# Layer 0 of a graph network: eight blocks per node tile divided anew between ScalarE and VectorE

## The chip, the cores and the metric

The kernel runs on one core of one Trainium2 chip. The metric is the device time of one execution in microseconds (us), as a median of three runs. Engine names follow the profile: PE is TensorE's matrix multiply and PEld its weight load, DVE is VectorE, ACT is ScalarE, POOL is GpSimd, SP is the queue of SyncE, which here only issues transfers. Unless a unit stands beside it, a time is in us.

## The reference, cut to what matters

Two layers of a graph network run over 8 batches, 2048 nodes and 64 features, all in float32. Layer 0 gives every node weights of its own, mixed from 16 matrices by the node's embedding.

```python
# layer 0: x (8, 2048, 64), A (2048, 2048), embedding (2048, 16), weight (16, 3, 64, 64)
w = einsum('nd,dkio->nkio', embedding, weight)
b = einsum('nd,do->no', embedding, bias)
As = [I, A, 2.0 * (A @ A) - I]
x_g = einsum('knm,bmc->bnkc', stack(As), x)
x = layernorm(x + einsum('bnki,nkio->bno', x_g, w) + b)
# layer 1: both supports are A
x1 = A @ x;  x2 = 2.0 * (A @ x1) - x
x = layernorm(x + concat([x, x1, x2, x1, x2]) @ weight1 + bias1)
```

The kernel takes x, A·x and A·(A·x) as its three operands of layer 0 and folds the 2 and the minus sign into the weights. It relies on the pattern of the matrix (every nonzero of a row has one value) and has a general path beside it for other matrices, which does not run on these inputs.

## The kernel before, in words

**Stages.** Four multiplications with the matrix ("hops") surround layer 0. The first hop (L254) takes the matrix in quarters and keeps sums of them. The second hop and the third are done by `seven_products` (L586), seven products of quarter size with eight steps each (L664). Between them stands layer 0, one tile of 128 nodes after the other, 16 tiles. The fourth hop (`hop_g`, `hop_tile`) and the last layer norm end the kernel.

**Operands of layer 0.** [...] every operand is divided into three parts: a high part, a low part and a mixed part. `parts` (L309) does that: ACT casts the high part (L312), DVE subtracts for the low part (L314), and the mixed part is made in one of two ways. With `quick` DVE does it in one instruction (L317); without, ACT scales the high part (L319) and POOL adds the low one (L320). `operands` (L725) prepares a tile's three operands: x (`of_x`, loaded as `xt`), the first hop (`of_hop`, after TensorE has transposed it, L300), and the second hop (`of_second`). Each is a generator that issues one step whenever it is called, and the tile before calls them.

**Blocks.** `mix0` (L402) runs eight blocks a tile. A block fills two banks of PSUM: `bank` (L84) takes one of four such pairs in turn, as they come free. There are two kinds of block.
- `by_batch` (L417), called for `(g, 0)` and `(g, 1)`: one pair of batches, eight of the 16 embedding entries, 18 matmuls of 512 columns. ACT evicts it in eight instructions of 128 elements, each scaled by the node's embedding entry, into tiles called `aside` (L423). When both blocks of `g` are there, POOL sums the aside tiles in three halvings (`sum_aside`, L440) and adds them to the sum `acc` (`add_aside`, L445).
- `by_four` (L425), called for `(g, 2)` to `(g, 5)`: two pairs of batches, four embedding entries, 36 matmuls of 256 columns. DVE evicts it in four instructions of 256 elements, each of which multiplies by the embedding entry and adds into `acc` (L433).

The loop over tiles gives the order of blocks in `pieces`, and in `at` the other work that is recorded ahead of each block. Tiles 0 to 14 have two blocks by batch and six by four, the last tile four and four:

```python
pieces = [(0, 0), (0, 4), (0, 5), (1, 2), (0, 1), (1, 3), (1, 4), (1, 5)]
```

**Order.** While layer 0 is recorded, the list `in_order` is set, and each engine keeps its instructions in the order in which they are recorded. `n1`, `n2`, `n3` are the steps of the previous tile's layer norm (L359: DVE sums and scales, POOL centres, ACT squares, DVE sums, ACT takes the root, DVE inverts, POOL normalises). `times_r` (L712) and `begin_sum` (L389) are POOL work for later tiles. `transpose` (L303) turns the previous tile's normalised values over for `project` (L458), which runs at a tile's end with two pairs of banks, and ACT copies its results out (L475).

**Third hop.** In `seven_products` the first step takes four pairs of banks, two for even products and two for odd ones:

```python
sums.extend([bank("accT") for _ in range(2)] for _ in range(2))
```

**Pools.** `RAW` buffers (5) hold raw matrix slabs, aside tiles and one pair of low and mixed parts a tile. `HL` buffers (8) hold high and low parts. `load_weights` puts layer 0's weights into raw buffers too.

Of the kernel before, what the change touches and what calls it, by code (L numbers as in the profile page):

```python
# [18 lines left out]
P = 128  # L19
B, N, C = 8, 2048, 64  # L20
NT = N // P
D = 16
DG = 4
EPS = 1e-5
FIRST = 8
HL = 8
RAW = 5
WARM = 12
SLOTS = 3
SPLIT = 4096.0  # L30
# [9 lines left out]
def pattern(  # L40
# [43 lines left out]
    def bank(name):  # L84

        return psum.tile([P, 2, 512], F32, tag="ps", name=name)
# [40 lines left out]
    def ordered(ins):  # L127
        if in_order:
            tc.keep_in_program_order(ins)
# [16 lines left out]

    def node_bias(pb):

        eT, b0_sb = bias_sb[:, : N // 4], bias_sb[:, N // 4 :]
        for j in range(4):  # L150
            for g in range(4):
                q = slice(32 * g, 32 * g + D)
                nc.tensor.matmul(  # L153
                    pb[g // 2][:, g % 2, j * C : (j + 1) * C], lhsT=eT[q, j * P : (j + 1) * P], rhs=b0_sb[q],
                    start=True, stop=True, tile_position=(32 * g, 0),
                )
# [2 lines left out]
        to = ebias[:, 8 * h : 8 * h + 8, :].rearrange("p (g t) c -> p g (t c)", g=2)  # L159
        ordered(nc.vector.tensor_copy(to, pb[h][:, :, : 4 * C]))  # L160

    wl = work2.tile([P, 5, C], F32, tag="t0", name="wl")
    bias_sb = work2.tile([P, N // 4 + C], F32, tag="t0", name="bias_sb")

    loads = [(bias_sb, bias), (pack_sb, pack[:, : NT * D]), (wl.rearrange("p k o -> p (k o)"), pack[:, NT * D + C :])]
    loads += [(bias1, pack[:, NT * D : NT * D + C]), (rrow, diag.to_broadcast([P, N]))]

    def weights():
# [230 lines left out]

    def mix0(t, tt, acc, at, pieces):  # L402

        def block(pm, lhsT, ds):
            for k in range(3):
                for n in range(3):
                    for j in range(2):
                        q = slice(j * C, (j + 1) * C)
                        nc.tensor.matmul(  # L409
                            pm[:, j], lhsT=tt[k][n][q, lhsT, :], rhs=w_parts[n][k][q, ds, :],  # L410
                            start=(k == 0 and n == 0), stop=(k == 2 and n == 2),
                        )

        def e(d):
            return emb_sb[:, t, d : d + 1]

        def by_batch(g, i):  # L417
            pm = bank("pm").rearrange("p j (d c) -> p j d c", c=C)
            block(pm, 2 * g + i, slice(0, 2 * DG))
            if i == 0:  # L420
                aside[g] = [rawp.tile([P, DG, 2, 2, C], F32, tag="raw", name="aside") for _ in range(2)]
            for d in range(2 * DG):
                ordered(nc.scalar.activation(aside[g][d // DG][:, d % DG, :, i, :], pm[:, :, d, :], AF.Copy, scale=e(d)))  # L423

        def by_four(g, dg):  # L425
            dg -= 2
            pm = bank("pm").rearrange("p j (i d c) -> p j i d c", i=2, d=DG)
            for i in range(2):
                block(pm[:, :, i], 2 * g + i, slice(dg * DG, (dg + 1) * DG))
            for d in range(DG):  # L430
                part = acc[:, 4 * g : 4 * g + 4, :]
                got = pm[:, :, :, d, :].rearrange("p j i c -> p (j i) c")
                ordered(nc.vector.scalar_tensor_tensor(part, got, e(dg * DG + d), part, ALU.mult, ALU.add))  # L433

        aside = {}

        def sum_aside(g):
            one, other = [a.rearrange("p d j i c -> p d (j i) c") for a in aside[g]]
            for to, more in ((one, other), (one[:, :2], one[:, 2:]), (one[:, 0], one[:, 1])):
                ordered(nc.gpsimd.tensor_tensor(to, to, more, ALU.add))  # L440

        def add_aside(g):
            part = acc[:, 4 * g : 4 * g + 4, :]
            one = aside[g][0][:, 0].rearrange("p j i c -> p (j i) c")
            ordered(nc.gpsimd.tensor_tensor(part, part, one, ALU.add))  # L445

        for n, (g, i) in enumerate([*pieces, (None, None)]):
            for work_here in at[n]:
                if isinstance(work_here, tuple):
                    for part in work_here[0]:  # L450
                        {"sum": sum_aside, "add": add_aside}[part](work_here[1])
                else:
                    work_here()
            if n < len(pieces):
                (by_batch if i < 2 else by_four)(g, i)
        return layernorm(acc)
# [126 lines left out]
        (S4, "B22", (0, 1)), ((0, 1), "B21", (0, 0)), ((1, 1), "T4", (1, 0)),  # L583
    )

    def seven_products(s, to, sums, more, wait=4, raw=()):  # L586

# [28 lines left out]
        def step(p, kk):  # L618
# [37 lines left out]

            def use(got):
                if p == 0 and kk == 0:
                    sums.extend([bank("accT") for _ in range(2)] for _ in range(2))
                acc, hl, S = sums[p % 2], got["hl"], got["s"]  # L660
                for i in range(2):
                    for h in range(2):
                        for c in range(2):
                            nc.tensor.matmul(  # L664
                                acc[i][:, c], lhsT=hl[h][:, i * P : (i + 1) * P], rhs=S[:, c * 512 : (c + 1) * 512],
                                start=(kk == 0 and h == 0), stop=(kk == KK - 1 and h == 1),
                            )
                if p == 3:
                    sum_of_y(kk, "T4")
                for f in more.get((p, kk), ()):  # L670
                    f()
                if kk < KK - 1:
                    return
                if p < 6:
                    todo.extend([nothing] * wait)
                for i in range(2):
                    for c in range(2):
                        todo.append(lambda i=i, c=c: put(acc[i][:, c], i, c))
                while p == 6 and todo:
                    todo.pop(0)()  # L680
                todo.extend(more.get(p, ()))
# [40 lines left out]
    def by_pair(a):  # L722
        return a.rearrange("p (j n) -> p j n", n=P)

    def operands(t, quick=False):  # L725

        xt = work2.tile([P, B // 2, P], F32, tag="t0", name="xt")
        load(nc.sync, xt, xT[t])
        tt = [None] * 3

        def begin(k, src):
            where, tag = ((rawp, "raw"), (spool, "s"))[k != 2]
            high = hpool.tile([P, B // 2, P], F32R, tag="hl", name="hl")
            pair = where.tile([P, 2, B // 2, P], F32R, tag=tag, name="parts")
            tt[k] = [high, pair[:, 0], pair[:, 1]]
            return parts(src, tt[k], by_half if k == 1 else lambda to: to, quick)

        def of_x():
            yield from begin(0, xt)

        def of_hop(pt=None):
            yield from begin(1, transposed(z[1][t], pt))

        def of_second():
            yield from begin(2, by_pair(z[2][t]))

        return tt, of_x(), of_hop, of_second()

# [74 lines left out]
    def quarter_back(a, b, which):  # L823
# [11 lines left out]
        (0, 6): [last_projected],  # L835
        **{(2 + t // KK, t % KK): [lambda t=t: add_bias(t)] for t in range(NT)},
        3: quarter_back(1, 1, 1), 4: quarter_back(0, 1, 0), 5: quarter_back(0, 0, 1),
    }, wait=2)

    third_got = {}  # L840

# [15 lines left out]
    for t in range(NT):  # L857
# [4 lines left out]
        if not last:  # L862
            following, of_x, of_hop, of_second = coming
            of_hop = of_hop()
            at[1] += [go(of_x)] * (1 if t else 3)
            at[2] += [go(of_hop), n1, go(of_hop), go(of_hop), n2]
            if t + 2 < NT:
                at[2] += [lambda: times_r(t + 2)]
                at[4] += [lambda: got.update(coming=operands(t + 2))]
            at[3] += [n3, go(of_second), lambda: got.update(acc=begin_sum(t + 1))]  # L870
            at[4] += [go(of_second), go(of_second)]
            at[6] += [(("sum", "add"), 0)]
            at[7] += [lambda: got.update(hT=transpose(h, "hT"))] if t else []
            pieces = [(0, 0), (0, 4), (0, 5), (1, 2), (0, 1), (1, 3), (1, 4), (1, 5)]
        else:
            at[1] += [n1, n2]
            at[2] += [n3, lambda: early(0, "y_high", *s)]
            at[3] += [(("sum",), 0), lambda: early(0, "y_low")]
            at[4] += [lambda: early(1, "y_high", *s)]
            at[5] += [lambda: early(1, "y_low")]  # L880
            at[6] += [(("add",), 0), lambda: got.update(hT=transpose(h, "hT")), lambda: early(2, "y_high")]
            at[7] += [(("sum",), 1), lambda: early(2, "y_low"), lambda: early(3, "y_high")]
            at[8] += [(("add",), 1), lambda: early(3, "y_low")]
            pieces = [(0, 0), (0, 1), (0, 4), (1, 0), (0, 5), (1, 1), (1, 4), (1, 5)]
        norm_now = mix0(t, tt, acc, at, pieces)
        if t:
            project(t - 1, got["hT"])
        if "coming" in got:
# [487 lines left out]
```

## Time and profile before

| What | Value |
|---|---|
| Three runs | 763.59, 763.61, 765.11; median 763.61 |
| Profiled execution, its own time | 764.04 |
| Its span, first to last instruction | 762.3 |
| Granted TensorE clock | 0.999 |
| Busy over the span | PE 753.6, PEld 660.6, DVE 560.2, ACT 406.7, POOL 269.7 |
| Busy in one steady tile of layer 0, 395.20 to 414.16 | PE 18.96, DVE 15.26, ACT 10.68, POOL 15.12 |
| DVE evictions in layer 0 (L433) | 376 of 482 ns, busy 181.0 |
| ACT evictions in layer 0 (L423) | 272, busy 74.0 |
| Start of the third hop on PE | 527.69 |

The span is what the trace covers; about 1.7 lie around it. Busy time is the union of an engine's instructions. The mean of one instruction can be longer than its share of busy time, because neighbours overlap: 272 evictions on ACT have a mean of 383 ns but are busy 74.0, so 272 ns each. Lines of the profile are those of the kernel before; the change adds lines, so L409 becomes L410 and L433 becomes L439 later on.

### The profile page before, as it was taken

To read this page: it belongs to the slowest core of one execution; us is meant where nothing else is said; L and a number is where in the kernel's file an instruction comes from. 1 tells how busy PE (TensorE), PEld (TensorE's weight loads), DVE (VectorE), ACT (ScalarE), POOL (GpSimd) and SP (SyncE) were. 2 spreads that over 40 slices of the span, in tenths; PEclk is the share of its full clock that TensorE was granted. 3 is DMA by queue.
4 is the path that set the end of the run, shared out by engine and by line. 5 is a ranking of instruction groups with operands and counts; after the bars stand their busy time and mean duration, and the time that the engine had idled before them with its cause. 6 is when DMAs were issued, how large, how long until landed. Compare 5 with 4: busy or idle time off the path is not lost.

```text
span 762.3 us, 16926 instructions
## 1 busy us (share of the span) xinstructions
PE 753.6 (99%) x6634; PEld 660.6 (87%) x6634; DVE 560.2 (73%) x1159; ACT 406.7 (53%) x896; POOL 269.7 (35%) x297
## 2 busy tenths in 40 slices
PE   9999999999999999999999999999999999999996
PEld 6888888888889999999999999998888888888885
DVE  6768867678757888888888888877688648668663
ACT  5456533877745555555555555558887663112111
POOL 0000000000026877777777777777100000011441
PEclk9999999999999999999999999999999999999999
DMA  8998996555520000000000000003454444565631
GB/s 325 346 393 282 350 312 233 154 177 162 171 69 17 20 20 15 20 18 16 16 16 17 15 16 3 2 16 87 135 167 151 130 154 142 175 177 175 208 127 46
DMA packets 73558, 96.69 MB, mean 127 GB/s; under 512 B 4864, under 2 KB 48384, under 8 KB 73344
## 3 DMA queue, kind: packets, MB, share of 16 engines
q1 hardware_dynamic: 62064, 76.66, 31.8%
q10 hardware_dynamic: 11408, 18.89, 6.6%
q8 instruction: 54, 0.88, 0.5%
q14 instruction: 32, 0.26, 0.1%
HBM read 76.65 MB, written 18.87 MB: 125 GB/s over the span
## 4 chain that ended last, share of the span: by engine, by line
PE 98%; DVE 1%; issue 0%; ACT 0%; DVEq 0%
PE pm L409 36%; PE accT L664 27%; PE acc L254 15%; PE a L254 10%; PE accT L254 6%; PE pu L466 2%; PE pt L300 1%; PE first L143 1%; PE accT L814 1%; DVE acc L433 1%; PE accT L466 0%; PE accT L153 0%; PE accT L300 0%; ACT sq L994 0%; DVE z L289 0%
## 5 line engine op out<-in xcount | busy, mean ns | idle before, releaser
L433 DVE SCALAR_TENSOR_TENSOR acc<-pm,pack_sb,acc 128x256 f32<-128x256 f32 x376 | 181.0, 482 | 44.0 <-PE pm L409 32.0
L409 PE MATMUL pm<-wh,hl 64*128 64x512 f32 (+1 forms) x1332 | 208.0, 303 | 0.0
L664 PE MATMUL accT<-s,hl 128*128 128x512 f32 x896 | 205.9, 390 | 0.8 <-DVE acc L433 0.8
L409 PE MATMUL pm<-wm,parts 64*128 64x512 f32 (+1 forms) x1332 | 203.5, 296 | 0.0
L409 PE MATMUL pm<-wl,parts 64*128 64x512 f32 (+1 forms) x1332 | 203.4, 296 | 0.0
L664 PEld LDWEIGHTS accT<-s,hl 128*128 128x128 f32 x896 | 167.5, 188 | 36.5 <-issue 1.6
L409 PEld LDWEIGHTS pm<-wh,hl 64*128 64x128 f32 x1332 | 130.9, 187 | 4.0 <-issue 0.4
L409 PEld LDWEIGHTS pm<-wl,parts 64*128 64x128 f32 x1332 | 130.8, 187 | 3.7
L409 PEld LDWEIGHTS pm<-wm,parts 64*128 64x128 f32 x1332 | 130.5, 187 | 3.8
L652 ACT CAST s<-raw 128x1024 fp32r<-128x1024 bf16 x104 | 109.9, 1057 | 37.9 <-ACT hl L234 23.4
L254 PE MATMUL acc<-hl,s 128*128 128x512 f32 x512 | 116.8, 390 | 0.0
L254 PEld LDWEIGHTS acc<-hl,s 128*128 128x128 f32 x512 | 96.2, 188 | 20.5 <-issue 0.3
L423 ACT ACTIVATE aside<-pm,pack_sb 128x128 f32<-128x128 f32 x272 | 74.0, 383 | 48.9 <-PE pm L409 48.1
L715 POOL TENSOR_TENSOR z<-z,rrow 128x512 f32<-128x512 f32 x16 | 21.1, 1320 | 212.4 <-DVE z L688 212.4
L234 ACT CAST hl<-z 128x256 fp32r<-128x256 f32 (+1 forms) x96 | 47.7, 515 | 60.1 <-PE acc L254 24.1
L440 POOL TENSOR_TENSOR aside<-aside 128x1024 f32<-128x1024 f32 (+2 forms) x51 | 75.3, 1476 | 4.2 <-ACT aside L423 1.6
L254 PE MATMUL a<-hl,s 128*128 128x512 f32 (+1 forms) x352 | 73.4, 370 | 0.0
L254 PEld LDWEIGHTS a<-hl,s 128*128 128x128 f32 x352 | 61.9, 188 | 11.3
L320 POOL TENSOR_TENSOR parts<-parts 128x512 fp32r<-128x512 f32 x45 | 58.2, 1294 | 35.1 <-DVE parts L314 27.5
L238 DVE TENSOR_TENSOR hl<-z,hl 128x512 fp32r<-128x512 f32 (+1 forms) x96 | 54.7, 577 | 12.9 <-ACT hl L234 10.1
L287 POOL TENSOR_TENSOR z<-z,got 128x512 f32<-128x512 f32 x3 | 4.8, 1631 | 144.4 <-ACT got L286 144.4
L254 PE MATMUL accT<-hl,s 128*128 128x512 f32 x192 | 44.3, 390 | 0.0
(136 smaller groups left out, 814.4 us busy)
## 6 DMA issues: line engine op xcount, KB each, us to landing
raw<-in_adj SPq DMA_DIRECT2D x58, 512.0 KB, 6.1
raw<-sums_of SPq DMA_DIRECT2D x64, 256.0 KB, 2.9
sums_of<-z ACTq DMA_DIRECT2D x16, 512.0 KB, 6.6
raw<-quarters SPq DMA_DIRECT2D x32, 256.0 KB, 2.7
raw<-in_adj SPq DMA_DIRECT2D x16, 384.0 KB, 3.5
quarters<-seen ACTq DMA_DIRECT2D x16, 256.0 KB, 5.8
xt<-in_xT SPq DMA_DIRECT2D x16, 256.0 KB, 2.7
z<-in_x SPq DMA_DIRECT2D x15, 256.0 KB, 6.8
```

The lines of the kernel that those rows point to most:

```text
L234: ordered(nc.scalar.copy(to[0], src))
L238: ordered(nc.vector.tensor_tensor(to[1], src, to[0], ALU.subtract))
L254: nc.tensor.matmul(accs[i], lhsT=s[:, i * P : (i + 1) * P], rhs=hl[h], start=(first and h == 0), stop=(last and h == 1),)
L320: ordered(nc.gpsimd.tensor_tensor(mixed, mixed, low, ALU.add))
L409: nc.tensor.matmul(pm[:, j], lhsT=tt[k][n][q, lhsT, :], rhs=w_parts[n][k][q, ds, :], start=(k == 0 and n == 0), stop=(k == 2 and n == 2),)
L423: ordered(nc.scalar.activation(aside[g][d // DG][:, d % DG, :, i, :], pm[:, :, d, :], AF.Copy, scale=e(d)))
L433: ordered(nc.vector.scalar_tensor_tensor(part, got, e(dg * DG + d), part, ALU.mult, ALU.add))
L440: ordered(nc.gpsimd.tensor_tensor(to, to, more, ALU.add))
L466: nc.tensor.matmul(pm[:, j, i * 3 * C : (i + 1) * 3 * C], lhsT=hT[q, 2 * g + i, :], rhs=v[q], start=True, stop=True,)
L652: ordered(nc.scalar.copy(s, got["raw"]))
L664: nc.tensor.matmul(acc[i][:, c], lhsT=hl[h][:, i * P : (i + 1) * P], rhs=S[:, c * 512 : (c + 1) * 512], start=(kk == 0 and h == 0), stop=( ...
L715: ordered(nc.gpsimd.tensor_tensor(to, to, r, ALU.mult))
```

## The change

Tiles 0 to 14 now have four blocks by batch and four by four. The blocks by batch of the second quarter of the batches and embedding entries (`g` = 1) go the new way: `mix0` gets `on_vector`, and for a `g` in it each block has one aside tile of its own, from which a single DVE reduce sums the eight entries over the outer axis, read with a step of 128 elements (`reduce_aside`). A DVE addition then adds the sums of both blocks to `acc` (`add_reduced`). The blocks by batch of `g` = 0 are summed on POOL as before. The last tile is as it was.

The mixed parts of x and of the second hop are always made by DVE (`quick`). The order of blocks and of the other work changes in tiles 0 to 14. In the third hop, the even products get the first and third pair of banks, the odd ones the second and fourth. `HL` is 7 and `RAW` is 6. The node bias is loaded in two transfers, the small one into a sixth slice of `wl`.

```diff
-HL = 8
-RAW = 5
+HL = 7
+RAW = 6
...
-    loads = [(bias_sb, bias), (pack_sb, pack[:, : NT * D]), (wl.rearrange("p k o -> p (k o)"), pack[:, NT * D + C :])]
+    loads = [(bias_sb, bias[:, : N // 4]), (wl[:, 5], bias[:, N // 4 :]), (pack_sb, pack[:, : NT * D])]
+    loads += [(wl[:, :5].rearrange("p k o -> p (k o)"), pack[:, NT * D + C :])]
...
-            if i == 0:
-                aside[g] = [rawp.tile([P, DG, 2, 2, C], F32, tag="raw", name="aside") for _ in range(2)]
+            if g in on_vector:
+                aside[g, i] = rawp.tile([P, 2 * DG, 2, C], F32, tag="raw", name="aside")
+                to = [aside[g, i][:, d] for d in range(2 * DG)]
+            else:
+                if i == 0:
+                    aside[g] = [rawp.tile([P, DG, 2, 2, C], F32, tag="raw", name="aside") for _ in range(2)]
+                to = [aside[g][d // DG][:, d % DG, :, i, :] for d in range(2 * DG)]
...
+        def reduce_aside(i):
+            if i == 0:
+                aside["sum"] = xcpool.tile([P, 2, 2, C], F32, tag="ln_xc", name="both")
+            src = aside[1, i].rearrange("p d j c -> p (j c) d")
+            to = aside["sum"][:, i].rearrange("p j c -> p (j c)")
+            ordered(nc.vector.tensor_reduce(to, src, AX.X, ALU.add))
+
+        def add_reduced(_):
+            part = acc[:, 4:8, :].rearrange("p (j i) c -> p i j c", j=2)
+            ordered(nc.vector.tensor_tensor(part, part, aside["sum"], ALU.add))
...
-                    sums.extend([bank("accT") for _ in range(2)] for _ in range(2))
+                    four = [bank("accT") for _ in range(4)]
+                    sums.extend([four[a], four[b]] for a, b in pairs)
...
-            yield from begin(0, xt)
+            yield from begin(0, xt, True)
...
-            yield from begin(2, by_pair(z[2][t]))
+            yield from begin(2, by_pair(z[2][t]), True)
...
-    }, wait=2)
+    }, wait=2, pairs=((0, 2), (1, 3)))
...
-            at[2] += [go(of_hop), n1, go(of_hop), go(of_hop), n2]
+            at[1] += [n1, lambda: got.update(acc=begin_sum(t + 1))]
             if t + 2 < NT:
-                at[2] += [lambda: times_r(t + 2)]
+                at[1] += [lambda: times_r(t + 2)]
+            at[1] += [n2, go(of_hop)]
+            at[2] += [n3, (("reduce",), 0), go(of_hop)]
+            at[4] += [go(of_hop), go(of_second)]
+            if t + 2 < NT:
                 at[4] += [lambda: got.update(coming=operands(t + 2))]
-            at[3] += [n3, go(of_second), lambda: got.update(acc=begin_sum(t + 1))]
-            at[4] += [go(of_second), go(of_second)]
-            at[6] += [(("sum", "add"), 0)]
+            at[5] += [(("reduce",), 1), (("add_reduced",), 1), go(of_second)]
+            at[6] += [(("sum",), 0)]
             at[7] += [lambda: got.update(hT=transpose(h, "hT"))] if t else []
-            pieces = [(0, 0), (0, 4), (0, 5), (1, 2), (0, 1), (1, 3), (1, 4), (1, 5)]
+            at[7] += [go(of_second)]
+            at[8] += [(("add",), 0)]
+            pieces, on_vector = [(1, 0), (0, 4), (1, 1), (0, 0), (0, 5), (0, 1), (1, 4), (1, 5)], (1,)
```

More of the change, by code (lines that the diff above doesn't have):

```diff
@@ L147, in node_bias @@
     def node_bias(pb):
-        eT, b0_sb = bias_sb[:, : N // 4], bias_sb[:, N // 4 :]
+        eT, b0_sb = bias_sb, wl[:, 5]
         for j in range(4):
@@ L160, in keep_node_bias @@
         ordered(nc.vector.tensor_copy(to, pb[h][:, :, : 4 * C]))
-    wl = work2.tile([P, 5, C], F32, tag="t0", name="wl")
-    bias_sb = work2.tile([P, N // 4 + C], F32, tag="t0", name="bias_sb")
-    loads = [(bias_sb, bias), (pack_sb, pack[:, : NT * D]), (wl.rearrange("p k o -> p (k o)"), pack[:, NT * D + C :])]
+    wl = work2.tile([P, 6, C], F32, tag="t0", name="wl")
+    bias_sb = work2.tile([P, N // 4], F32, tag="t0", name="bias_sb")
+    loads = [(bias_sb, bias[:, : N // 4]), (wl[:, 5], bias[:, N // 4 :]), (pack_sb, pack[:, : NT * D])]
+    loads += [(wl[:, :5].rearrange("p k o -> p (k o)"), pack[:, NT * D + C :])]
     loads += [(bias1, pack[:, NT * D : NT * D + C]), (rrow, diag.to_broadcast([P, N]))]
@@ L398, in begin_sum, with mix0 @@
         return acc
-    def mix0(t, tt, acc, at, pieces):
+    def mix0(t, tt, acc, at, pieces, on_vector=()):
         def block(pm, lhsT, ds):
@@ L419, in by_batch @@
             block(pm, 2 * g + i, slice(0, 2 * DG))
-            if i == 0:
-                aside[g] = [rawp.tile([P, DG, 2, 2, C], F32, tag="raw", name="aside") for _ in range(2)]
+            if g in on_vector:
[5 more added lines that the diff above has]
+                to = [aside[g][d // DG][:, d % DG, :, i, :] for d in range(2 * DG)]
             for d in range(2 * DG):
-                ordered(nc.scalar.activation(aside[g][d // DG][:, d % DG, :, i, :], pm[:, :, d, :], AF.Copy, scale=e(d)))
+                ordered(nc.scalar.activation(to[d], pm[:, :, d, :], AF.Copy, scale=e(d)))
         def by_four(g, dg):
@@ L445, in add_aside @@
             ordered(nc.gpsimd.tensor_tensor(part, part, one, ALU.add))
+        def reduce_aside(i):
[7 more added lines that the diff above has]
+            ordered(nc.vector.tensor_tensor(part, part, aside["sum"], ALU.add))
+        does = {"sum": sum_aside, "add": add_aside, "reduce": reduce_aside, "add_reduced": add_reduced}
         for n, (g, i) in enumerate([*pieces, (None, None)]):
@@ L450, in mix0 @@
                     for part in work_here[0]:
-                        {"sum": sum_aside, "add": add_aside}[part](work_here[1])
+                        does[part](work_here[1])
                 else:
@@ L584, in pattern, with seven_products @@
     )
-    def seven_products(s, to, sums, more, wait=4, raw=()):
+    def seven_products(s, to, sums, more, wait=4, raw=(), pairs=((0, 1), (2, 3))):
         kept = {}
@@ L729, in operands, with begin @@
         tt = [None] * 3
-        def begin(k, src):
+        def begin(k, src, quick):
             where, tag = ((rawp, "raw"), (spool, "s"))[k != 2]
@@ L738, in of_x @@
         def of_x():
-            yield from begin(0, xt)
+            yield from begin(0, xt, True)
         def of_hop(pt=None):
-            yield from begin(1, transposed(z[1][t], pt))
+            yield from begin(1, transposed(z[1][t], pt), quick)
         def of_second():
-            yield from begin(2, by_pair(z[2][t]))
+            yield from begin(2, by_pair(z[2][t]), True)
         return tt, of_x(), of_hop, of_second()
@@ L883, in pattern @@
             at[8] += [(("add",), 1), lambda: early(3, "y_low")]
-            pieces = [(0, 0), (0, 1), (0, 4), (1, 0), (0, 5), (1, 1), (1, 4), (1, 5)]
-        norm_now = mix0(t, tt, acc, at, pieces)
+            pieces, on_vector = [(0, 0), (0, 1), (0, 4), (1, 0), (0, 5), (1, 1), (1, 4), (1, 5)], ()
+        norm_now = mix0(t, tt, acc, at, pieces, on_vector)
         if t:
```

## The prediction

> **What bounds the kernel now.** I read the page first: busy time, then the chain of waits, then the groups of instructions by form, then one tile of layer 0 as a timeline. All times are us unless marked ns.
>
> ```profile
> PE 753.6 (99%) x6634; PEld 660.6 (87%) x6634; DVE 560.2 (73%) x1159; ACT 406.7 (53%) x896; POOL 269.7 (35%) x297
> PE 98%; DVE 1%; issue 0%; ACT 0%; DVEq 0%
> PE pm L409 36%; PE accT L664 27%; PE acc L254 15%; PE a L254 10%; PE accT L254 6%; PE pu L466 2%; PE pt L300 1%; PE first L143 1%; PE accT L814 1%; DVE acc L433 1%; PE accT L466 0%; PE accT L153 0%; PE accT L300 0%; ACT sq L994 0%; DVE z L289 0%
> ```
>
> The chain is matmul work almost throughout, so a change pays only if it shortens the stream of matmuls or one of its few gaps. Layer 0 (`pm`, L409) is 36% of it. Now the start times of three neighbours in a steady tile (columns: start, duration of the merged row, engine, line, operation):
>
> ```profile
> 404.18 0.40 PE L409 MATMUL pm<-wh,hl 64*128 64x512 f32 x2
> ...
> 406.25 0.28 PE L409 MATMUL pm<-wh,hl 64*128 64x256 f32 x2
> ...
> 410.56 0.41 PE L300 MATMUL pt<-ident,xc 64*128 64x64 f32 x8
> ```
>
> From 404.18 to 406.25 runs one block by batch, 18 matmuls of 512 columns: 2.07. From 406.25 to 410.56 run two blocks by four, 36 matmuls of 256 each: 4.31, or 2.155 a block. Both compute equally much. Durations of single matmuls (303 ns as a mean) overlap, so start-to-start times are what I use. The whole tile, 395.20 to 414.16, has PE busy for all its 18.96; DVE is busy 15.26, ACT 10.68, POOL 15.12. Nothing waits on TensorE's side there.
>
> The one gap is at the start of the third hop:
>
> ```profile
> 527.47 2.03 DVE L433 SCALAR_TENSOR_TENSOR acc<-pm,pack_sb,acc 128x256 f32<-128x256 f32 x4
> 527.16 1.75 ACT L475 COPY z<-pu 128x256 f32<-128x256 f32 x6 [1.28 <-PE pu L466]
> 527.69 1.20 PE L664 MATMUL accT<-s,hl 128*128 128x512 f32 x4
> 529.65 0.70 PE L664 MATMUL accT<-s,hl 128*128 128x512 f32 x2 [0.76 <-DVE acc L433]
> ```
>
> Four matmuls go into the first bank from 527.69. At 227 ns each (400 take 90.89 in the chain) the fifth could start at 528.60; it starts at 529.65, after the last tile's final four evictions (527.47 to 529.50). That gap costs 1.05.
>
> [...] 680 ns for 512 elements (L362), like a two-input operation of that size (682 to 692 ns). [...] no VectorE operation of before steps its inner axis by more than one element, so no trace shows it yet. [...] the subtraction for the second hop (L314, `parts<-z,hl`), issued while POOL works, takes 1122 ns, the same for `xt` 692 ns.
>
> **The change part by part.**
>
> *Blocks.* In tiles 0 to 14 two blocks by four become blocks by batch (four and four instead of two and six; the last tile already has this form). TensorE saves 2 × (2.155 − 2.07) = 0.17 a tile, 15 × 0.17 = **2.6**. The new period, if nothing waits, is 18.96 − 0.17 = 18.79.
>
> *ACT.* It gains 16 evictions of 128 (74.0 busy over 272 is 0.272 each, 4.35) and loses two scaled copies (about 0.66 each): 10.68 + 4.35 − 1.3 = 13.7 of 18.79. It fits.
>
> *POOL.* It loses two additions of 512 (1.29 each): 15.12 − 2.6 = 12.5. It fits.
>
> *DVE.* It loses 8 evictions (0.482 each, 3.86). It gains two mixed parts (0.69 each, L317), one addition of 256 (0.42) and two reduces of 1024 elements down to 128. I name the time of one reduce R. Low bound: 1.22, what a two-input operation of 1024 elements takes (L204, 1225 ns). High bound: every element lies 512 bytes from the last, [...] the streaming part of 1.07 doubles and R = 2.29; halving is my choice of an end, no source gives it. I take 1.22, since nothing measured shows a penalty on this engine. Busy: 15.26 − 3.86 + 1.38 + 0.42 + 2.44 = 15.6 of 18.79. That fits, but order matters more than load.
>
> *The ring that could bind.* The built program shows which bank each block takes and what it waits for. The fifth block of a tile, (0,5), takes the bank of the second, (0,4), hence waits for its four evictions; (0,1) takes the bank of the transposed hop, hence waits for the subtraction that reads it; the next tile's transposition waits for the evictions of (1,5). I follow one round from the start of (0,5) at 0.
> - TensorE: (0,5) to 2.16, (0,1) to 4.23, (1,4) to 6.38, transposition, (1,5) to 8.82, projection; the next tile starts at 9.98.
> - ACT's evictions of (0,1) start 0.22 after it (397.42 to 397.64 in the trace) and last 2.17: 6.62. POOL's first sum (2.4) ends at 9.1.
> - DVE: evictions of (0,5) from 2.37 (0.21 behind TensorE, as at 413.21), second reduce, addition, subtraction, free at 6.5; evictions of (1,4) from 6.59 to 8.6. The mixed part then waits for POOL's first sum, and ends at 9.65. Evictions of (1,5) end at 11.6.
> - POOL, held up 0.45 by the mixed part: two more sums (1.28, 0.74) and the addition (0.75) end at 12.4.
> - DVE: the subtraction for `xt` waits for that POOL addition, 13.0; sum, scaling, mixed part of `xt`, 14.4. POOL's centring is behind the mixed part, 15.3; ACT squares, 16.0; DVE sums them, 16.7; then evicts (0,4), 18.64. TensorE follows 0.14 later (529.51 to 529.65): **18.78**.
>
> The ring takes 18.78 where TensorE alone takes 18.79. So I expect almost no stall, and little room: 0.2 more on it returns all of the blocks' gain. I allow 0.02 a tile for errors, 0.3 in all. The low bound of this cost is 0, the high bound belongs to the rivals.
>
> *The reduces on it.* The second one has room of 0.5, because the mixed part behind it waits for POOL anyway. The first stands ahead of the subtraction that frees the bank of (0,1): it ends R + 0.5 after the start of (0,5), plus 0.14 to reach TensorE, against 2.16. It fits while R is below 1.5.
>
> *Third hop.* The first product takes banks one and three of four. The third was the first projection's, which ACT has copied out by about 528.0 (half of 1.75 from 527.16), before 528.60. **1.05** is saved. What is late next: the transposition of the last tile in step (0,5), at 539.8 now, 538.8 then; it needs POOL's normalised tile, ready at 538.0 (536.78 plus 1.22). So it keeps its gain.
>
> *Pools, loads, order.* One buffer fewer for high and low parts: in the first hop a step's low part now waits for the matmuls of three steps before instead of four; a step takes 3.6, so two steps remain, and cost 0. [...] One raw buffer more removes ACT's wait of 0.79 for POOL in the last tile, which is off the path: 0. The split bias load is one more SP issue of 64 columns behind three earlier loads, needed only in the second hop: 0. `times_r` and the start of the next sum move earlier on POOL, behind the centring, into time it has free.
>
> **Sum.** −2.6 − 1.05 + 0.3 = −3.35 against the profiled execution's 764.04 (span 762.3 and 1.7 around it). That execution is 0.43 above the median of 763.61, and I apply the difference to the median: **760.3**.
>
> **Rivals.**
> - *The ring eats the gain.* If it runs 0.17 longer, say because DVE is blocked once more by POOL, tiles take 18.96 as before and only the third hop's 1.05 remains: 762.6. [...] Against it: POOL has 2.6 less to do. Between this and the forecast lies a continuum.
> - *The strided reduce is slow.* The first reduce with R = 2.29 holds (0,1) up by 0.78; following the round again gives 19.6. That is 0.64 a tile over now, 15 × 0.64 = 9.6, less 1.05: 772.2. It turns the sign at R = 1.75, where the stall of 0.24 equals 0.17 and the third hop's share. For it: [...] 512 bytes between elements. Against it: [...] no row shows such a loss.
> - *The blocks gain nothing on TensorE.* If the weight loads that go with 512 columns set the pace, only 1.05 is saved, as above; against it, the last tile already has four blocks of 512, and the three that don't follow a projection take 2.05 to 2.07.
>
> **How the numbers follow.** No stall or small ones, below 762.1: 0.70. About 0.2% of the time, 1.5, is what a measurement can tell from no change. The eaten gain, 762.1 to 765.1: 0.12. Slower, above 765.1, nearly all by the reduce: 0.18. The forecast alone would range from 759.3 to 762.0; the low end is the sum without the allowance and 0.7 for noise. The range runs on to 766, through the eaten gain and a mildly slow reduce, and leaves out the slow end (about 0.13) and 0.04 below.
>
> **What would show it.** Right: a steady tile of 18.8 in the chain, the group of the reduce near 1220 ns, no DVE or POOL piece in the chain inside layer 0, fewer than 0.3 of idle time on `pm`, and a third hop that starts without DVE. Wrong: a reduce above 1500 ns, TensorE waiting for L315 at every (0,1), or for L439 at every (0,5).

## The result, and the profile after

The changed kernel takes 773.99 (median of four runs, 773.82 to 775.22); the kernel before took 764.19 beside it (763.59 to 765.11). The ratio is 1.0131, with a 95% interval of 1.0113 to 1.0148. It is slower by 9.8, where 760.3 was forecast and 766.0 was the upper end of the range.

The page of the changed kernel, busy time, then the chain that ended last by engine, then two groups (line, engine, operation, out<-in, shapes, count, busy, mean ns, idle before):

```profile
PE 758.6 (98%) x6094; PEld 644.5 (83%) x6094; DVE 587.8 (76%) x1114; ACT 453.4 (59%) x1106; POOL 239.7 (31%) x267
...
PE 42%; DVE 8%; issue 7%; ACT 6%; POOL 4%; DMA 0%; POOLq 0%; DVEq 0%
...
L429 ACT ACTIVATE aside<-pm,pack_sb 128x128 f32<-128x128 f32 x512 | 137.5, 401 | 32.1 <-PE pm L410 32.1
...
L458 DVE TENSOR_REDUCE both<-aside 128x128 f32<-128x1024 f32 x30 | 59.2, 1973 | 0.0
```

Before, the chain was 98% TensorE. Now it leaves TensorE through DVE, ACT and POOL. (Its shares no longer add up to 100% here, so I use it for its engines and not for sums.) The last line is the reader's first find: the strided reduce takes **1973 ns**, not the 1220 that the forecast took.

The chain in a steady tile, 400.63 to 420.01, shows how that reaches TensorE (columns: start, duration, piece):

```profile
406.81 0.69 DVE ss L371
407.50 0.40 DVE acc L439
...
408.97 0.48 DVE acc L439
409.45 0.06 DVE ln_r L375
409.51 1.83 issue
411.34 0.69 DVE parts L315
412.03 0.04 issue
412.07 4.49 PE pm L410 x54
```

The "issue" piece of 1.83 is the reduce: it waits for nothing, it just runs (409.48 to 411.42 in the timeline). Behind it stands the subtraction L315, which frees the bank that block (0,1) needs, and TensorE starts that block at 412.07, at once when the subtraction ends. In the rows of TensorE's timeline, each a pair of matmuls, the tile has two holes: 0.41 from the row at 409.19 to the next, where 0.23 is usual ((0,5) waits for the evictions of (0,4)), and 0.37 from the row at 411.70, where 0.12 is usual ((0,1) waits for L315). The first rows after the holes are spaced wider as well (0.19 instead of 0.12, 0.34 instead of 0.23). Together that is 0.6, the whole excess of a 19.39 tile over the forecast's 18.79.

Start times of tiles and of the third hop give 9.5 of the loss (span 762.3 to 772.0, that is 9.7):

| Stretch | Before | After | Difference |
|---|---|---|---|
| Start of layer 0 | 226.17 | 226.38 | +0.21 |
| Tiles 0 and 1 | 36.31 | 38.47 | +2.16 |
| Tiles 2 to 14 | 246.48 (18.96 each) | 252.08 (19.39 each) | +5.60 |
| Last tile, to the third hop's first matmul | 18.72 | 19.44 | +0.72 |
| From there to the start of the last matmul | 227.64 | 228.46 | +0.82 |

Most of what tiles 0 and 1 lose is one wait in tile 1: 2.11 between two matmul starts at 252.33, ahead of (0,5). The last two lines have a cause of their own. The chain at the last tile's end, in the same columns:

```profile
525.90 2.59 POOL aside L446
528.49 0.02 issue
528.51 2.69 DMA raw<-corner
531.20 0.02 issue
531.23 1.05 ACT s L670
532.27 2.07 ACT aside L429 x8
534.34 0.47 ACT hT L307
...
539.03 0.14 issue
539.17 1.83 PE accT L683 x7
```

An early load for the third hop (`raw<-corner`) waits for POOL's first halving, because it goes into the buffer which that halving reads. ACT's cast L670 waits for the load, and the evictions, `hT` and the projection come late behind it. The fifth matmul of the third hop follows the first after 2.79, where it was 1.96.

### The profile page after: what moved, and what is told of

It reads as the page before. It is cut to its first block, busy times and chain, and to the rows that moved or that the text cites. A ratio compares the mean times of both kernels' runs of the same rounds, so it can differ in the third digit from the quotient of the medians.

```text
span 772.0 us, 16020 instructions
## 1 busy us (share of the span) xinstructions
PE 758.6 (98%) x6094; PEld 644.5 (83%) x6094; DVE 587.8 (76%) x1114; ACT 453.4 (59%) x1106; POOL 239.7 (31%) x267
## 4 chain that ended last, share of the span: by engine, by line
PE 42%; DVE 8%; issue 7%; ACT 6%; POOL 4%; DMA 0%; POOLq 0%; DVEq 0%
PE accT L683 13%; PE pm L410 12%; PE a L255 9%; PE accT L255 6%; DVE acc L439 4%; ACT z L493 3%; POOL xc L366 3%; DVE ss L371 1%; DVE parts L315 1%; ACT sq L354 1%; DVE s L363 1%; PE pu L484 1%; POOL aside L446 1%; ACT hl L313 1%; PE accT L833 1%
## 5 line engine op out<-in xcount | busy, mean ns | idle before, releaser
L410 PE MATMUL pm<-wh,hl 64*128 64x256 f32 (+1 forms) x1152 | 193.4, 328 | 3.2 <-DVE ln_r L375 1.7
L410 PE MATMUL pm<-wm,parts 64*128 64x256 f32 (+1 forms) x1152 | 186.2, 316 | 0.0
L410 PE MATMUL pm<-wl,parts 64*128 64x256 f32 (+1 forms) x1152 | 186.2, 315 | 0.0
L429 ACT ACTIVATE aside<-pm,pack_sb 128x128 f32<-128x128 f32 x512 | 137.5, 401 | 32.1 <-PE pm L410 32.1
L670 ACT CAST s<-raw 128x1024 fp32r<-128x1024 bf16 x104 | 109.9, 1057 | 39.0 <-ACT hl L235 28.4
L439 DVE SCALAR_TENSOR_TENSOR acc<-pm,pack_sb,acc 128x256 f32<-128x256 f32 x256 | 123.5, 482 | 10.9 <-PE pm L410 3.7
L410 PEld LDWEIGHTS pm<-wh,hl 64*128 64x128 f32 x1152 | 111.9, 187 | 18.8 <-issue 4.9
L410 PEld LDWEIGHTS pm<-wm,parts 64*128 64x128 f32 x1152 | 111.6, 186 | 7.9
L410 PEld LDWEIGHTS pm<-wl,parts 64*128 64x128 f32 x1152 | 111.8, 186 | 6.5
L255 PEld LDWEIGHTS acc<-hl,s 128*128 128x128 f32 x512 | 96.1, 188 | 20.8 <-ACT hl L235 0.6
L458 DVE TENSOR_REDUCE both<-aside 128x128 f32<-128x1024 f32 x30 | 59.2, 1973 | 0.0
L493 ACT COPY z<-pu 128x256 f32<-128x256 f32 x90 | 26.3, 401 | 32.2 <-PE pu L484 32.2
```

The source lines that it names most:

```text
L255: nc.tensor.matmul(accs[i], lhsT=s[:, i * P : (i + 1) * P], rhs=hl[h], start=(first and h == 0), stop=(last and h == 1),)
L410: nc.tensor.matmul(pm[:, j], lhsT=tt[k][n][q, lhsT, :], rhs=w_parts[n][k][q, ds, :], start=(k == 0 and n == 0), stop=(k == 2 and n == 2),)
L429: ordered(nc.scalar.activation(to[d], pm[:, :, d, :], AF.Copy, scale=e(d)))
L458: ordered(nc.vector.tensor_reduce(to, src, AX.X, ALU.add))
L493: ordered(nc.scalar.copy(to[k], got[:, :, :, 2 - k, :]))
L670: ordered(nc.scalar.copy(s, got["raw"]))
```

## The experiments

My theory after the result: the step of 512 bytes makes the reduce slow, and its place ahead of L315 turns that into waits of TensorE; the tile 1 stall, the last tile and the third hop are separate small losses. Rivals: a reduce to 128 sums of eight is slow however it reads; or DVE has too much to do, wherever the reduce stands; or DVE and POOL get in each other's way.

**Reading in line.** Only the reduce's access pattern changes; it sums neighbours, so this run leaves out the right grouping.

```diff
-            src = aside[1, i].rearrange("p d j c -> p (j c) d")
+            src = aside[1, i].rearrange("p d j c -> p (d j c)").rearrange("p (n d) -> p n d", d=2 * DG)
```

> The changed kernel, but the DVE reduce (L458) reads its 1024 elements in the order in which they lie, eight neighbours per sum, instead of with a step of 128 elements. It leaves out the right grouping: the sums of the second quarter are over the wrong entries. Number of elements, sums, instructions and waits are the same. Theory (the step costs the time): the reduce falls from 1973 ns to about 1225, no tile waits for it, a tile of layer 0 takes 18.8 to 18.9 instead of 19.39, and 15 tiles return 7.5 to 9 (with the stall of tile 1): 765 to 767. Rival (a reduce to 128 sums of eight is slow however it reads): it stays at 1.9 to 2.0 and the kernel at 774. Rival (TensorE is held up by DVE and POOL getting in each other's way, not by the reduce): the reduce falls, but tiles stay above 19.2 and the kernel above 771.

Measured: 765.41, ratio 1.0016 (1.0010 to 1.0023). The operation by itself (count, minimum, median and maximum in ns):

```profile
L458 DVE TENSOR_REDUCE both<-aside x30: 1164/1207/1212, 234.1 to 502.5; 128x128 f32<-128x1024 f32 x30
```

Tiles take 18.84 on average. The step costs 0.78 a reduce, and with nothing else changed it costs the kernel 8.6 of its 9.8. Both rivals named for this run fall as causes of the whole loss. The third, DVE's load, does not: a faster reduce is also less load.

**How long a step is slow?** Three kernels, which leave out the right grouping too, read with steps of 2, 4 and 16 elements: `"p (n d c) -> p n c d"` with c = 2, 4 and 16, in place of the outer axis. One run each.

> The changed kernel with the reduce reading its 1024 elements with a step of 2 elements (8 bytes) instead of 128 (512 bytes), in the order of two interleaved sums; it leaves out the right grouping of the second quarter's sums. Theory [...] the reduce takes about half of the surplus, 1.6. Rival (any step but one element costs all of it): 1.97. Rival [...] 1.21 or little more.

> As the run with a step of 2 elements, with 4 elements (16 bytes). It leaves out the same grouping. Theory [...] 1.97. Rival (only long steps are slow): 1.2 to 1.6.

> As the run with a step of 2 elements, with 16 elements (64 bytes). It leaves out the same grouping. Theory [...] as with 16 bytes, 1.97. Rival (only long steps are slow): between the 16-byte run and 1.97.

Measured: 765.56, 774.27 and 773.16. The operation in the run with 2, then with 4, then with 16 elements:

```profile
L458 DVE TENSOR_REDUCE both<-aside x30: 1164/1207/1212, 234.7 to 503.1; 128x128 f32<-128x1024 f32 x30
```

```profile
L458 DVE TENSOR_REDUCE both<-aside x30: 1957/1985/2035, 234.8 to 510.9; 128x128 f32<-128x1024 f32 x30
```

```profile
L458 DVE TENSOR_REDUCE both<-aside x30: 1885/1936/1964, 234.7 to 510.1; 128x128 f32<-128x1024 f32 x30
```

8 bytes cost nothing, 16 bytes cost everything, and 512 bytes (1988 median in the changed kernel) no more. No single text had that: my theory was right at 16 and 64 bytes but expected half the surplus at 8, and the rival that had 8 bytes free expected 16 bytes to be cheap as well. Why the change comes between 8 bytes (1207 ns) and 16 (1985 ns) no run shows. The time of the kernel follows the reduce: 765.4 to 765.6 with 1207 ns, 773 to 774 with 1936 to 1988.

**The step on the writer's side.** ACT writes the eight entries next to one another (a step of 32 bytes), the reduce reads in line, the result is the same.

```diff
-                aside[g, i] = rawp.tile([P, 2 * DG, 2, C], F32, tag="raw", name="aside")
-                to = [aside[g, i][:, d] for d in range(2 * DG)]
+                aside[g, i] = rawp.tile([P, 2, C, 2 * DG], F32, tag="raw", name="aside")
+                to = [aside[g, i][:, :, :, d] for d in range(2 * DG)]
```

> The changed kernel with the step moved from the reader to the writer: the aside tile holds the eight entries next to one another, ACT's evictions write 128 elements with a step of 8 (32 bytes), and the reduce reads in line. The result is the same. Theory: the reduce takes about 1225 ns as in the run that reads in line; if ACT writes with a step at the same speed (0.27 each), the kernel takes 765 to 767. Rival (the step costs ACT as much as it cost DVE): 256 of ACT's evictions take up to twice as long, ACT's 13.8 of a tile grows by up to 4.3, the evictions by batch run late and tiles stay above 19.2, 771 or more.

Measured: 765.40, ratio 1.0008 (0.9999 to 1.0016). The reduce's median is 1207 ns. ACT's 512 evictions are busy 139.9 instead of 137.5; 240 of them write with the step, so it costs 0.01 each (in a steady tile ACT is busy 13.92 instead of 13.78, with 16 of them). The mean of one rises from 401 to 456 ns, so it adds to the time an eviction takes to finish, but hardly to ACT's load. Theory confirmed. With the reduce at the size that I had forecast, the kernel is as fast as before, though, and not 3.4 faster; the chain in tile 1 shows the largest of the other losses:

```profile
248.97 1.38 POOL xc L366
250.35 0.02 issue
250.38 0.64 ACT sq L354
251.02 0.02 issue
251.04 0.69 DVE ss L371
251.73 0.40 DVE acc L439
...
253.68 0.12 DVE ln_r L375
253.80 0.03 issue
253.83 2.18 PE pm L410 x32
```

From the start of (0,5) in tile 0 (235.08) to that in tile 1 (253.83) is 18.75, the ring of the forecast almost to the hundredth. But tile 0 has no projection, so TensorE is there after 16.98 and waits 1.76.

**The subtraction first.** The changed kernel, with L315 ahead of the first reduce.

```diff
-            at[2] += [n3, (("reduce",), 0), go(of_hop)]
+            at[2] += [n3, go(of_hop), (("reduce",), 0)]
```

> The changed kernel with one exchange: the subtraction for the first hop's low part (L315), which frees the bank of block (0,1), is issued ahead of the first reduce instead of behind it. The reduce stays strided and slow. Theory (it is the place of the slow reduce that holds TensorE up): the wait of (0,1) for L315 goes, (0,5) may keep part of its wait for the evictions of (0,4); a tile takes 18.8 to 19.1, the kernel 765 to 769. Rival (the load of DVE, 17.1 busy in 19.4, binds wherever the reduce stands): the stall moves to the evictions of (0,5), which are then behind the reduce; a tile stays at 19.3 to 19.5, the kernel at 773 to 775.

Measured: **783.81**, ratio 1.0244 (1.0226 to 1.0262); tiles take 20.9 to 21.0 or 19.2 to 19.3, mostly by turns. Both texts missed. The next run shows why.

**Evicting (0,4) first.** The changed kernel; the sum of squares is recorded behind (0,4).

```diff
-            at[1] += [n2, go(of_hop)]
-            at[2] += [n3, (("reduce",), 0), go(of_hop)]
+            at[1] += [go(of_hop)]
+            at[2] += [n2, n3, (("reduce",), 0), go(of_hop)]
```

> The changed kernel with its slow strided reduce and one exchange: the norm's sum of squares and root are recorded behind block (0,4) instead of ahead of it, so DVE evicts (0,4) before it waits for the sum of squares. Theory (the round runs through the order of DVE's queue, not through DVE's load): (0,5) no longer waits for the norm; the sum of squares ends 6.9 after a tile's start, root 7.6, reduce 9.6, subtraction 10.2, and TensorE needs it at 10.9, so no tile waits in the steady state: 18.8 a tile instead of 19.39. In tile 1 the stall falls from 2.1 to about 0.7. 764 to 766. Rival (the load of DVE, 17.1 of 19.4, with a reduce of 1.97 that nothing moves): tiles stay at 19.2 to 19.4, 770 to 774.

Measured: 783.06, ratio 1.0237 (1.0218 to 1.0256). The waits at (0,5) and, in the steady state, at (0,1) are gone as expected, yet from the third tile on nine of 13 tiles take 20.4 to 20.9, the other four 19.2. In the timeline of DVE:

```profile
398.06 2.01 DVE L458 TENSOR_REDUCE both<-aside 128x128 f32<-128x1024 f32 x1
400.11 0.42 DVE L462 TENSOR_TENSOR acc<-acc,both 128x256 f32<-128x256 f32 x1
400.45 2.92 DVE L315 TENSOR_TENSOR parts<-z,hl 128x512 fp32r<-128x512 f32 x1
403.29 2.03 DVE L439 SCALAR_TENSOR_TENSOR acc<-pm,pack_sb,acc 128x256 f32<-128x256 f32 x4
```

and in that of POOL:

```profile
400.43 2.39 POOL L446 TENSOR_TENSOR aside<-aside 128x1024 f32<-128x1024 f32 x1 [1.58 <-ACT aside L429]
```

(The bracket is POOL's idle time ahead of it and what ended that.) DVE reaches the second hop's subtraction 0.02 after POOL has begun the first of three halvings, and the subtraction takes 2.92 instead of 0.68. The evictions of (1,4) and (1,5) are behind it, and TensorE waits for them at the next tile's start (1.67 between two matmul starts at most tiles). The run with the subtraction first has the same row, 2.92 at 402.20, beside a halving that began at 402.18. Another tile of the run that evicts (0,4) first shows the other outcome, in DVE and in POOL:

```profile
442.20 0.68 DVE L315 TENSOR_TENSOR parts<-z,hl 128x512 fp32r<-128x512 f32 x1
442.19 2.94 POOL L446 TENSOR_TENSOR aside<-aside 128x1024 f32<-128x1024 f32 x1 [1.59 <-ACT aside L429]
```

Here the subtraction starts 0.01 after the halving, keeps its 0.68, and it is the halving that takes longer. From the third tile on the two runs divide without exception. Where the subtraction starts 20 to 29 ns behind the halving, it takes 2.91 to 2.93 and the tile 20.4 to 21.0; where it starts 9 to 19 ns behind, it takes 0.68, the halving 2.94 to 2.96 and the tile 19.2 to 19.3. So the collision is what makes these tiles slow. The subtraction takes 2.24 longer, nearly the whole of the halving beside it (2.39), and ends 0.55 after it (403.37 against 402.82). By the recorded starts POOL is first in both outcomes; what decides between them was not shown. In the changed kernel itself the subtraction started at 416.37, ahead of the halving at 416.71, and took 0.68. The halving follows block (0,1), so the stall at (0,1) held it back; both runs that took this stall away ran into the collision.

**Moving the subtraction out of the way.** From the last run, L315 for the second hop goes ahead of the second reduce, and the addition behind the mixed part.

```diff
-            at[5] += [(("reduce",), 1), (("add_reduced",), 1), go(of_second)]
+            at[5] += [go(of_second), (("reduce",), 1)]
...
-            at[7] += [go(of_second)]
+            at[7] += [go(of_second), (("add_reduced",), 1)]
```

> The run that evicts (0,4) first (783), whose reduce is still the slow strided one, with two DVE operations moved: the subtraction for the second hop's low part goes ahead of the second reduce instead of behind it and its addition, and that addition goes behind the mixed part. Load and durations stay. Theory (that run is slow because DVE reaches the subtraction 0.02 after POOL has begun its first halving of 1024, and then waits 2.2 for it): the subtraction takes 0.7 to 1.5 instead of 2.92, tiles take 18.8 to 19.0 instead of 20.9, the kernel 764 to 768, below the changed kernel in spite of the slow reduce. Rival (DVE has too much to do with a reduce of 1.97, in whatever order): tiles stay at 19.3 or more, 773 to 783.

Measured: **793.18**, ratio 1.0368 (1.0351 to 1.0386). The subtraction falls to 1.31 as expected, but most tiles take 20.7 to 20.8. My theory failed on the time; the rival had the tile (19.3 or more) but not the kernel (773 to 783). The chain repeats every 20.76 (381.71 to 402.47); its middle:

```profile
383.75 1.23 DVE parts L315
384.98 1.94 DVE both L458
386.92 0.40 DVE acc L439
...
388.87 1.46 DVE parts L318
390.33 0.90 DVE acc L462
...
393.38 0.14 issue
393.51 0.46 PE pt L301 x8
393.97 8.48 PE pm L410 x108
402.45 0.02 issue
402.47 0.49 DVE acc L439
```

DVE goes through three sets of evictions with the subtraction, the reduce, the mixed part and the addition between them: 11.7 in a row. Then TensorE, which waited for the last set, needs 8.9 to reach the next (0,5), which DVE needs. The subtraction was taken out of one collision, and three shorter ones came instead: subtraction 1.31 (0.68 alone), mixed part 1.54 (0.68), addition 0.96 (0.43), 2.0 in all. So with the same DVE operations the tile depends on their order (19.39, 19.2 to 20.9, 20.7 to 20.8), and the one collision is not all of it: in this run the length of DVE's stretch between the evictions of (0,5) and (1,5) sets the time, and a slow reduce is one piece of it. That a kernel with the slow reduce and no collisions would run at 18.8 (20.76 less 2.0) is an estimate that no run tried. From the third tile on, no tile with the slow reduce came under 19.2, so DVE's load isn't ruled out as a cause of what would be left.

**The pairs of banks alone.** The kernel before, with `pairs=((0, 2), (1, 3))` for the third hop.

> The kernel before with one part of the change alone: even products of the third hop get the first and third pair of banks, odd ones the second and fourth. The forecast's step: the fifth matmul of the third hop follows the fourth at once, 0.9 after the first instead of 1.96, and 1.05 is saved, 763.1. Rival (the pairs of banks are handed out in the order in which they come free, and the first product gets the pair of block (1,5), evicted last, either way): the start is as before, 1.96 between first and fifth matmul, and the time within 0.2 of the kernel before.

Measured: 764.61, ratio 0.9998 (0.9990 to 1.0006). The time excludes the 1.05 (a ratio of 0.9986) but not half a microsecond; the trace shows that the mechanism is absent: the fifth matmul still waits for L433. In the profiled execution it came even later, 2.69 after the first, since a transfer for ACT's cast was 0.73 late there. Whether other executions have that wait isn't shown.

**Buffers back, and three repairs.** First RAW = 5 on top of the step on ACT's writes.

> The run with the step moved to ACT's writes (765.4), with RAW at 5 as in the kernel before; HL stays 7. Theory (with 6 buffers the second early load of the last tile lands in a buffer that POOL's first sum still reads; with 5 it lands where an early load was read long ago): ACT's cast does not wait for a transfer, the last tile takes 18.7 instead of 19.3, the fifth matmul of the third hop follows the first after 1.96 instead of 2.8: 764.0. Rival (one buffer fewer moves the wait to the aside tiles inside layer 0): tiles grow above 18.9, or the last tile keeps its 19.3; 765.2 or more.

Measured: 764.26, ratio 0.9999 (0.9990 to 1.0008), which is 1.14 less than without. The last tile takes 18.73 and the fifth matmul follows after 1.96. Confirmed, at 1.14 where 1.4 was expected. With (0,4) evicted first as well:

> Three repairs together: the step on ACT's writes, RAW at 5, and (0,4) evicted ahead of the norm's sum of squares. Theory: the stall of 1.76 at the fifth block of tile 1 (one round of 18.75 against a TensorE stream of 17.0, since tile 0 has no projection) goes as well; 764.0 less 1.7 is 762.3. Rival (the stall in tile 1 only moves on to (0,1), which waits for the subtraction at the end of the same round): about 1 of it stays, 763.3 to 764.

Measured: 761.97, ratio 0.9968 (0.9959 to 0.9978). Tiles 0 and 1 together take 36.1 instead of 37.74, the steady tile 18.76. The same exchange cost 9 with the slow reduce: here DVE starts the subtraction at 408.23, ahead of POOL's halving at 409.00, and it takes 0.68.

**The start of the third hop.** One recorded step moves behind the last evictions.

```diff
-            at[7] += [(("sum",), 1), lambda: early(2, "y_low"), lambda: early(3, "y_high")]
-            at[8] += [(("add",), 1), lambda: early(3, "y_low")]
+            at[7] += [(("sum",), 1), lambda: early(3, "y_high")]
+            at[8] += [(("add",), 1), lambda: early(2, "y_low"), lambda: early(3, "y_low")]
```

> The three repairs, and in the last tile the low part for the third hop's third step is recorded behind the evictions of block (1,5) instead of ahead of them. Theory (the start of the third hop waits for these evictions because DVE first waits about 1.0 for that low part): the fifth matmul of the third hop follows the first after 1.0 instead of 1.96, about 1.0 less than the run of the three repairs: 761.3. Rival (the evictions wait for the block itself): no difference. Rival (the third step then waits for its low part): the wait shows again within the first three steps, no difference.

Measured: **761.10**, ratio 0.9960 (0.9946 to 0.9974), faster than both kernels. The chain from 522 to 530 holds nothing but TensorE:

```profile
522.00 1.72 PE pm L410 x29
523.72 1.30 PE pu L484 x16
525.02 5.04 PE accT L683 x21
```

The fifth matmul follows the first after 1.04.

## Why the prediction was wrong, point by point

- **The blocks: right.** 18.79 a tile was forecast where nothing waits; with a fast reduce it is 18.84 (765.4 and 765.6), with all repairs 18.76. The saving of 0.17 a tile was measured as 0.12 to 0.20.
- **Loads: right but for the reduce.** In a steady tile ACT is busy 13.78 (13.7 forecast) and POOL 13.08 (12.5; it is held up more often than I counted: its first halving has a mean of 2609 ns where it was 2411). DVE is busy 17.08 where 15.6 was forecast; the two reduces explain 2 × 0.75 of it, and in the last run of the experiments DVE is busy 15.63.
- **The reduce: the mis-sized term.** I bounded it at 1.22 and 2.29, took 1.22 and measured 1.97. (The 1.07 of streaming in the upper bound comes out of the trace as twice the step from 692 ns for 512 elements to 1225 for 1024; its doubling was my estimate, and the surplus turned out as 0.75.) The choice failed in its reason: "nothing measured shows a penalty" was true of a trace without any such access, so it spoke for neither end, and the 1.22 came from an operation that reads in line. This step cost most: 0.75 too little for each reduce, and 8.6 of the kernel's 9.8.
- **What a slow reduce does: right in kind.** The rival with R = 2.29 gave 19.6 a tile and 772.2; at 1.97 it is 19.39 and 774.0. The place (L315 ahead of (0,1), and (0,5) behind (0,4)) is the one named, and R lies above 1.75, where I put the change of sign. I gave it too small a chance. That 772.2 lies so near the result is luck in part. The rival's own rule at R = 1.97 gives a stall of 0.45, a tile of 19.24 and 766.8; the wait of (0,5), the first round, the raw buffers and the third hop's missing gain, all outside that rule, make up the rest.
- **The ring: right in size, applied to too few tiles.** 18.78 forecast, 18.75 measured. (Counted from the start of (0,5) in the run with the step on ACT's writes.) Part of that is luck: POOL's addition ended at 12.84 instead of 12.4, and the centring began before the mixed part of x was through instead of behind it (248.97, against 249.43); the two errors about cancel. I set the ring against the steady stream of TensorE alone. In the first round that stream is 16.98, and 1.76 is lost once (2.11 in the changed kernel). The waits of DVE for POOL that the ring counts show in the changed kernel: beside POOL the mixed part at 418.92 takes 0.94 and the subtraction for `xt` at 422.00 takes 1.18, where 0.68 to 0.69 is usual.
- **Third hop: the step failed.** I took the third of four banks for the projection's. The fifth matmul still follows the last eviction of (1,5), by 0.14 with the new pairs (529.98 to 530.12 in the run with the pairs alone) as before, so the first product still has that bank. Most likely banks are handed out in the order in which the program comes to use them, and not as they are listed; no run shows that by itself. The 1.05 itself was real: with one DVE operation moved the fifth matmul came at 1.04, and the kernel gained 0.87.
- **Buffers "at 0": wrong for RAW.** I followed who waits inside ACT and didn't ask which buffer the early load would land in. With RAW at 6 it lands behind POOL's halving; undoing that brought 1.14. HL at 7 was not tried alone; no wait in the runs points to it.
- **The range.** With R right at 1.22 the kernel takes 765.4, which is inside the range, so the reduce alone put the result outside it. But 765.4 is not the 760.3 of the forecast: the tile 1 stall (1.8), RAW (1.1) and the missing third-hop gain (about 1) use up what the blocks bring. So the most likely case, faster, failed on several steps, each of a size that alone would have been small.

## What to carry to other kernels

Before a DVE operation gets a new access pattern, write down its step in bytes, and if no trace of the kernel has such a step, price it at the slow end. (Here a reduce of 1024 float32 elements took 1207 ns with 4 and 8 bytes, and 1936 to 1988 with 16, 64 and 512; ACT's writes with 32 bytes cost 0.01 each.) Where engines run in a fixed order, write down the longest stretch that one of them goes through between two hand-overs and try it in the first and last round as well as the steady one, with the collisions of DVE and POOL in it: a repair that shifts DVE against POOL by a few tenths can cost more than what it repaired (783.81 and 783.06 here, against 773.99). For a changed number of buffers, ask which earlier reader the next early load will stand behind.

## What the runs showed that I had not expected

- A reduce of 1024 float32 elements takes 1207 ns with a step of 4 or 8 bytes, and 1936 to 1988 with 16, 64 or 512: a threshold between 8 and 16 bytes, not a slope.
- ACT's writes with a step of 32 bytes cost 0.01 each in load, where DVE's reads with 16 bytes or more cost 0.73 to 0.78 per 1024 elements.
- A few nanoseconds went with who waited: started 20 to 29 ns behind a POOL halving of 1024, a DVE subtraction took 2.91 to 2.93 instead of 0.68; started 9 to 19 ns behind, it kept its 0.68 and the halving took 2.94 to 2.96 instead of 2.39. The tile took 20.4 to 21.0 or 19.2 to 19.3 accordingly.
